# Attention products of four steps issued together instead of two, with twelve transposed-weight tiles and a smaller arena

## The chip, the cores and the metric

The kernel runs on one core of a Trainium2 chip. The metric is device time in microseconds (us) from the start to the end of one launch, taken as the median of several runs. Names of engines are those of the profile: PE is TensorE's matmul, PEld its weight loads, DVE is VectorE, ACT is ScalarE, POOL is GpSimd, SP is SyncE, whose queue issues most of the transfers.

## What is computed

Four transformer blocks follow one another on x of 8 batches x 112 tokens x 256 channels. All read the same context of 8 x 375 x 192. Cut to what matters (layer norms, biases and residual sums are in each part):

```python
def attention(x, ctx, wq, wk, wv, wo, bo):            # 16 heads
    q, k, v = heads(x @ wq), heads(ctx @ wk), heads(ctx @ wv)
    attn = softmax(einsum('bhid,bhjd->bhij', q, k) * scale)
    return merge(einsum('bhij,bhjd->bhid', attn, v)) @ wo + bo
# blocks 0 and 1: heads of 64 channels
h = h + attention(ln1(h), ln1(h), ...)                # self, 112 keys
h = h + attention(ln2(h), context, ...)               # cross, 375 keys
h = h + (lin * gelu(gate)) @ w2                       # feed-forward, 2 x 1024 wide
# block 2: cross attention alone, heads of 64 channels
# block 3: heads of 16 channels: masked self attention, masked cross attention, MLP of 1024
```

Everything is in 32-bit floats.

## The kernel before

Tokens lie as 896 rows in seven tiles of 128. Stages are numbered: 0 self, 1 cross, 2 feed-forward (block 0); 3, 4, 5 the same for block 1; 6 the cross attention of block 2; 7 self, 8 cross and 9 MLP of block 3.

Attention is cut into 176 *steps*. A self step of blocks 0 and 1 is one batch and eight heads; a cross step is one batch and four heads. Steps 0 to 15 are stage 0, 16 to 47 stage 1, 48 to 63 stage 3, 64 to 95 stage 4. From step 96 stage 6 runs with steps of stage 7 in between, from step 138 stage 8 with the rest of stage 7. Each step is made of four pieces:

- S, the scores (L948): matmuls into a PSUM tile `s` (two buffers of two banks). Behind them stand, in program order, the softmax: maxima on DVE (L910, or L896 with a mask), exponentials on ACT (L916, L904), reciprocals on DVE, and scaling of the weights `pr` on POOL, one head at a time for 375 keys (L925), one step at a time for 112 keys (L931). Heads of 16 channels are scaled after the products instead.
- T, the transposes (L975) of `pr` into a PSUM tile `mm` (four buffers), copied by ACT or DVE into a tile `wT` (L347, L355, L981, L984): three `wT` tiles for a cross step, two for a self step of eight heads.
- PV, the products with the values (L1005): 12 matmuls for a cross step of four heads. Then the result is copied into `oT`.
- E, the second half of the exponentials where heads have 16 channels.

Scores multiply pieces of 64 rows (32 in block 3), products write 64 columns (32), and the other matmuls use the whole array of 128 x 128.

PE's order is written out by the kernel's own planner (`Plan`). A loop over the steps calls S of step i + 2, then PV, then T of step i + 1, then E of step i + 2. Between these it calls `fill`, which takes *items* from a list of other work: projections to queries and keys (L665, L687), values (L712), keys of the context (L753 and L762), values of the context (L787 and L796), output projections with the residual sum and the next layer norm (L631, L635, L566 to L576), layer-norm transposes (L597), feed-forward (L1223). An item has a cost, a due step and items it must follow, with a least distance in the planner's own clock; `pace` sets how much is taken per step, and `ready` picks the item that is due first and can go. Key and value jobs of the context are opened ahead of a step's scores and closed in the next turn. Feed-forward items must follow the scores of the segment's last step by 3 us of that clock (L1238 to L1245). The loop runs in three segments, which end at the feed-forward of block 0 (step 48), of block 1 (step 96), and at the MLP; what is left of a segment's work is placed in the next.

Queries, keys and values live in one SBUF tile, `arena`, of 128 partitions x 12224 columns. The planner gives each a range of columns (values from the top, the others from the bottom: `find`, L109) and takes it back once the last reader has been issued. An item without room is not ready. Weights go through seven buffers of their own, loaded by SP in a fixed order as buffers come free.

The core of the loop, where the change is:

```python
            if lo <= i + 2 < hi:
                plan.main(("S", i + 2))

            if lo <= i < hi and (i - lo) % 2 == 1:
                plan.main(("PV", i - 1))
                plan.main(("PV", i))
            if lo <= i + 1 < hi:
                n = steps[i + 1]
                share = left / (n + 2)
                left -= plan.fill(2 * share)
                for k in range(n):
                    plan.main(("T", i + 1, k))
```

Of the kernel before, what the change touches and what calls it, by code (L numbers as in the profile page):

```python
# [299 lines left out]
def kernel(ctx: ExitStack, tc: tile.TileContext, a: dict, out: bass.AP):  # L300
    nc = tc.nc
    PSUM = bass.MemoryType.PSUM
    RINGS = {"w": 7, "row": 2, "xn": 3}
    ARENA = 12224

    const = ctx.enter_context(tc.tile_pool(name="const", bufs=1))
    wpool = ctx.enter_context(tc.tile_pool(name="wpool", bufs=RINGS["w"]))
    rpool = ctx.enter_context(tc.tile_pool(name="rpool", bufs=RINGS["row"]))
    ppool = ctx.enter_context(tc.tile_pool(name="ppool", bufs=4))
    tpool = ctx.enter_context(tc.tile_pool(name="tpool", bufs=6))  # L310
    xpool = ctx.enter_context(tc.tile_pool(name="xpool", bufs=RINGS["xn"]))
    small = ctx.enter_context(tc.tile_pool(name="small", bufs=4))
    ps_s = ctx.enter_context(tc.tile_pool(name="ps_s", bufs=2, space=PSUM))
# [5 lines left out]

    arena = const.tile([P, ARENA], F32, name="arena")  # L320
    plan = Plan(RINGS, ARENA, lambda k: 512 if k[0] == "v" else S if k[0] == "k" and k[1] in (1, 4, 6, 8) else 4 * T)

# [806 lines left out]
    def first_of(st, b):  # L1129
        return at[(st, b, 0)]  # L1130
# [263 lines left out]
    for seg in range(3):  # L1394
        lo, hi = cuts[seg], cuts[seg + 1]

        for s in (lo, lo + 1):
            for k in plan.items[("S", s)].uses + plan.items[("PV", s)].uses:
                mk = plan.maker.get(k)
                if mk is None or plan.items[mk].done:  # L1400
                    continue
                if plan.items[mk].begin is not None:
                    plan.require(mk)
                else:
                    plan.drain(mk)
        for i in range(lo - 2, hi):
            plan.step = i
            left = plan.pace(i, seg)
            plan.close_jobs()
            if lo <= i + 2 < hi:  # L1410
                plan.main(("S", i + 2))

            if lo <= i < hi and (i - lo) % 2 == 1:
                plan.main(("PV", i - 1))
                plan.main(("PV", i))
            if lo <= i + 1 < hi:
                n = steps[i + 1]
                share = left / (n + 2)
# [3 lines that stand above are left out]
                    left -= plan.fill(min(left, share))  # L1422
            if ("E", i + 2) in plan.items and lo <= i + 2 < hi:
                plan.main(("E", i + 2))
            plan.fill(left)
            plan.open_jobs(1 if i + 1 >= first_of(8, 0) else 2, i + 3.5, seg)
# [38 lines left out]
```

## Time and profile before

| what | value |
|---|---|
| time, median of 3 runs | 1659.37 us (1658.89 to 1661.41) |
| the profiled execution | 1662.19 us, its span 1660.3 us |
| PE busy | 1635.5 us, 99% of the span |
| PEld, DVE, ACT, POOL busy | 1143.1, 809.9, 782.9, 719.6 us |
| scores, transposes, products on PE (L948, L975, L1005) | 211.7, 235.4, 179.5 us |
| scaling of the weights on POOL (L925) | 384 x 1.241 us |
| mean granted PE clock | 0.997 |

The span is the time from the first to the last instruction of one profiled execution. "Busy" of PE counts overlapping matmuls once, and their ends are modelled. A row of the timeline gives the start, the length from there to the last end, the engine, the line of the code, the operation, output and inputs, and after an x the number of instructions; in square brackets stands how long the engine was idle ahead of it and what ended the idle time. A 32-bit matmul leaves two records on PE, a transpose one. A row of a table by stretch gives the stretch, its length, busy time of PE, PEld, DVE, ACT and POOL with the number of instructions, the granted PE clock (1 is full speed), the busy share of the transfer engines, and GB/s.

### The profile page before, as it was taken

How to read it: one execution, taken by the hardware profiler on the slowest of the kernel's cores; microseconds unless marked ns; L12 is line 12 of the kernel's file. 1: busy time of each engine (PE TensorE's matmuls, PEld its weight loads, DVE VectorE, ACT ScalarE, POOL GpSimd, SP SyncE). 2: the span in 40 equal slices, each digit the busy share in tenths (PEclk: the TensorE clock that was granted, in tenths of full speed). 3: DMA queues.
4: the chain of work that ended last, by engine and by line, in shares of the span. 5: the costliest groups of instructions: out<-in, count | busy, mean ns of one | idle time of the engine just before them, and what ended most of it. 6: DMA issues, size and time to landing. Idle time of an engine off the chain costs nothing.

```text
span 1660.3 us, 30115 instructions
## 1 busy us (share of the span) xinstructions
PE 1635.5 (99%) x11772; PEld 1143.1 (69%) x11772; DVE 809.9 (49%) x2163; ACT 782.9 (47%) x2450; POOL 719.6 (43%) x689
## 2 busy tenths in 40 slices
PE   8999999999999999999999999999999999999999
PEld 7877666666666878676666665666666666766667
DVE  3444445444532244544454552244455556678752
ACT  3554344444431444444444452144445555687772
POOL 1323455646631233355565580364564447422110
PEclk9999999999999999999999999999999999999999
DMA  5012020000101011000000010100000000000000
GB/s 187 5 50 57 3 87 1 1 26 1 51 30 45 1 30 52 27 1 30 1 2 26 1 46 29 33 22 2 1 2 1 16 1 27 30 2 2 2 2 23
DMA packets 26566, 39.50 MB, mean 24 GB/s; under 512 B 1544, under 2 KB 21560, under 8 KB 26424
## 3 DMA queue, kind: packets, MB, share of 16 engines
q1 hardware_dynamic: 25495, 36.74, 7.0%
q8 instruction: 93, 1.52, 0.4%
q10 hardware_dynamic: 864, 0.79, 0.2%
q14 instruction: 50, 0.40, 0.1%
q0 software_dynamic: 64, 0.05, 0.0%
HBM read 35.88 MB, written 0.92 MB: 22 GB/s over the span
## 4 chain that ended last, share of the span: by engine, by line
PE 91%; ACT 3%; DVE 3%; POOL 2%; issue 1%; DMA 0%; ACTq 0%; DVEq 0%; POOLq 0%
PE mm L631 13%; PE mm L665 11%; PE mm L1005 10%; PE s L948 10%; PE mm L975 10%; PE mm L753 8%; PE mm L787 7%; PE mm L1223 6%; PE mm L762 5%; PE mm L796 4%; PE mm L712 4%; ACT pr L904 2%; PE mm L1258 2%; POOL pr L925 1%; PE mm L597 1%
## 5 line engine op out<-in xcount | busy, mean ns | idle before, releaser
L925 POOL TENSOR_SCALAR pr<-pr,rinv 112x375 f32<-112x375 f32 x384 | 468.7, 1241 | 335.9 <-DVE rinv L922 335.7
L916 ACT ACTIVATE pr<-s,nm 112x375 f32<-112x375 f32 (+1 forms) x640 | 302.0, 489 | 168.7 <-DVE nm L910 166.5
L355 DVE COPY arena<-mm 128x375 f32<-128x375 f32 (+4 forms) x187 | 111.9, 608 | 295.4 <-PE mm L762 137.5
L975 PEld LDWEIGHTS mm<-ident,pr 112*128 112x128 f32 (+2 forms) x1920 | 209.3, 151 | 52.3 <-issue 20.9
L975 PE MATMUL mm<-ident,pr 112*128 112x112 f32 (+2 forms) x1920 | 235.4, 264 | 8.6 <-ACT pr L904 3.3
L910 DVE TENSOR_REDUCE nm<-s 112x2 f32<-112x750 f32 (+1 forms) x224 | 206.3, 957 | 70.6 <-PE s L948 67.2
L347 ACT COPY arena<-mm 128x375 f32<-128x375 f32 (+4 forms) x181 | 94.0, 519 | 298.6 <-PE mm L762 139.6
L948 PE MATMUL s<-arena 64*112 64x375 f32 (+3 forms) x1792 | 211.7, 394 | 0.1
L1005 PEld LDWEIGHTS mm<-wT,arena 128*64 128x64 f32 (+5 forms) x3840 | 159.9, 129 | 36.9 <-issue 21.2
L347 ACT COPY wT<-mm 128x448 f32<-128x448 f32 (+2 forms) x232 | 122.3, 535 | 122.6 <-PE mm L975 122.6
L1005 PE MATMUL mm<-wT,arena 128*64 128x112 f32 (+5 forms) x3840 | 179.5, 261 | 0.0
L948 PEld LDWEIGHTS s<-arena 64*112 64x112 f32 (+1 forms) x1792 | 114.0, 173 | 80.5 <-issue 31.2
L931 POOL TENSOR_TENSOR pr<-pr,rinv 112x896 f32<-112x896 f32 x32 | 53.9, 1684 | 210.5 <-DVE rinv L929 199.6
L904 ACT ACTIVATE pr<-pr,nm 112x112 f32<-112x112 f32 (+1 forms) x256 | 124.7, 490 | 33.5 <-DVE nm L896 33.5
L916 ACT ACTIVATION_READ_ACCUMULATOR pr<-s,nm 112x1 f32 x640 | 133.3, 208 | 0.0
L572 POOL TENSOR_TENSOR rs<-ve,mhalf 128x1 f32<-128x1 f32 x70 | 39.6, 567 | 193.0 <-DVE ve L570 192.8
L922 DVE RECIPROCAL rinv<-sums 112x1 f32<-112x1 f32 x384 | 62.3, 162 | 89.8 <-ACT pr L916 89.3
L787 PE MATMUL mm<-L_xattn_Wv,ctxA 128*128 128x512 f32 (+1 forms) x192 | 92.2, 600 | 2.0 <-ACT wT L347 1.3
L753 PE MATMUL mm<-ctxA,L_xattn_Wk 128*128 128x375 f32 x256 | 92.5, 485 | 0.0
L635 DVE TENSOR_TENSOR x<-mm,x 128x256 f32<-128x256 f32 x70 | 29.6, 422 | 113.7 <-PE mm L631 113.7
L665 PE MATMUL mm<-hT,L_xattn_Wq 128*128 128x224 f32 x384 | 84.1, 363 | 0.1
L355 DVE COPY wT<-mm 128x448 f32<-128x448 f32 (+2 forms) x120 | 73.6, 613 | 16.7 <-PE mm L975 16.3
(135 smaller groups left out, 2296.3 us busy)
## 6 DMA issues: line engine op xcount, KB each, us to landing
L_xattn_Wo<-in_L_xattn_Wo_dram SPq DMA_DIRECT2D x3, 1024.0 KB, 16.7
L_xattn_w_ff<-in_L_xattn_w_ff_dram SPq DMA_DIRECT2D x3, 1024.0 KB, 5.2
L_xattn_Wv<-in_L_xattn_Wv_dram SPq DMA_DIRECT2D x4, 512.0 KB, 6.0
L_xattn_Wq<-in_L_xattn_Wq_dram SPq DMA_DIRECT2D x2, 1024.0 KB, 4.7
L_xattn_Wp<-in_L_xattn_Wp_dram SPq DMA_DIRECT2D x2, 1024.0 KB, 5.7
L_xattn_wq<-in_L_xattn_wq_dram SPq DMA_DIRECT2D x2, 1024.0 KB, 4.7
L_xattn_wo<-in_L_xattn_wo_dram SPq DMA_DIRECT2D x2, 1024.0 KB, 5.5
L_xattn_mlp_w<-in_L_xattn_mlp_w_dram SPq DMA_DIRECT2D x2, 1024.0 KB, 5.2
```

Source lines behind the costliest of these rows:

```text
L347: nc.scalar.copy(dst, src)
L355: nc.vector.tensor_copy(dst, src)
L631: nc.tensor.matmul(ps[:, :D], lhsT=oT[:, c, t * P : (t + 1) * P], rhs=got[wv or w][:, c, :], start=(c == 0), stop=(c == n - 1),)
L665: nc.tensor.matmul(ps[:, i * 2 * T : (i + 1) * 2 * T], lhsT=got[w][:, k, m * P : (m + 1) * P], rhs=hT[:, k, lo:hi], start=(k == 0), stop=( ...
L753: nc.tensor.matmul(ps[:, :S], lhsT=got[wv][:, (2 * u + i) * P : (2 * u + i + 1) * P], rhs=ctxA[:, cols], start=True, stop=False,)
L787: nc.tensor.matmul(ps[: KCH[c][1], :], lhsT=lhs(ctxA, slice(0, KA), c), rhs=got[w][:, hf * 512 : (hf + 1) * 512], start=True, stop=False,)
L910: nc.vector.tensor_reduce(nm[:, :, :ns], sv, AX.X, ALU.max, negate=True)
L916: nc.scalar.activation(pr[:, bk, sl, :], sv[:, bk, sl, :], AF.Exp, bias=nm[:, bk, sl : sl + 1], accum_out=sums[:, bk, sl : sl + 1],)
L925: nc.gpsimd.tensor_scalar_mul(pr[:, bk, sl, :], pr[:, bk, sl, :], rinv[:, bk, sl : sl + 1])
L948: nc.tensor.matmul(tiles[i][:, n % 2, (n // 2) * nk : (n // 2 + 1) * nk], lhsT=qap(h), rhs=kap(h), start=True, stop=True,)
L975: nc.tensor.transpose(pt[:kl, m * T : (m + 1) * T], cell[h][:, c * P : c * P + kl], ident[:T, :T])
L1005: nc.tensor.matmul(po[p0 : p0 + dp, blk * T : (blk + 1) * T], lhsT=got[vk][:kl, hv * dp : (hv + 1) * dp], rhs=wt, start=(c == 0 and par(h) ...
```

## The change

Products of a step are no longer issued in each second turn of the loop. They are collected in a list, which is emptied when it holds four steps, at the end of a segment, and, from the first step of stage 8 on, in each second turn as before. `wT` gets twelve buffers instead of six, and the arena gets 9536 columns instead of 12224. Nothing that is computed changes.

```diff
-    ARENA = 12224
+    ARENA = 9536
...
-    tpool = ctx.enter_context(tc.tile_pool(name="tpool", bufs=6))
+    tpool = ctx.enter_context(tc.tile_pool(name="tpool", bufs=12))
...
+        waiting = []
         for i in range(lo - 2, hi):
             plan.step = i
             left = plan.pace(i, seg)
...
             if lo <= i + 2 < hi:
                 plan.main(("S", i + 2))
 
-            if lo <= i < hi and (i - lo) % 2 == 1:
-                plan.main(("PV", i - 1))
-                plan.main(("PV", i))
+
+            if lo <= i < hi:
+                waiting.append(("PV", i))
+                if len(waiting) == 4 or i + 1 == hi or (i >= first_of(8, 0) and (i - lo) % 2 == 1):
+                    while waiting:
+                        plan.main(waiting.pop(0))
             if lo <= i + 1 < hi:
                 n = steps[i + 1]
```

## The prediction

> **What bounds the kernel now.** I read the page's busy times and chain first, to see which engine sets the end.
>
> ```profile
> span 1660.3 us, 30115 instructions
> PE 1635.5 (99%) x11772; PEld 1143.1 (69%) x11772; DVE 809.9 (49%) x2163; ACT 782.9 (47%) x2450; POOL 719.6 (43%) x689
> PE 91%; ACT 3%; DVE 3%; POOL 2%; issue 1%; DMA 0%; ACTq 0%; DVEq 0%; POOLq 0%
> ```
>
> TensorE (PE) has 99% of the span and 91% of the chain. Its instructions run in the order written, so this change, which only moves work, counts in two ways: less matmul time, or more waits of PE. Next I read PE and GpSimd (POOL) in time where the first segment ends: step 47 of 176 is its last, and the feed-forward follows.
>
> ```profile
> 460.69 1.35 PE L975 MATMUL mm<-ident,pr 112*128 112x112 f32 x12
> 461.97 1.52 PE L948 MATMUL s<-arena 64*112 64x375 f32 x8
> 463.42 2.53 PE L1005 MATMUL mm<-wT,arena 128*64 128x112 f32 x48
> 465.88 0.60 PE L975 MATMUL mm<-ident,pr 112*128 112x112 f32 x4
> ...
> 474.90 1.35 PE L975 MATMUL mm<-ident,pr 112*128 112x112 f32 x12
> 476.17 2.06 PE L1005 MATMUL mm<-wT,arena 128*64 128x112 f32 x38
> ```
>
> ```profile
> 459.82 3.66 POOL L925 TENSOR_SCALAR pr<-pr,rinv 112x375 f32<-112x375 f32 x3
> 463.44 0.57 POOL L572 TENSOR_TENSOR rs<-ve,mhalf 128x1 f32<-128x1 f32 x1
> 464.13 1.23 POOL L574 TENSOR_SCALAR xn<-x,mv,rs 128x256 f32<-128x256 f32 x1
> 465.44 0.73 POOL L576 TENSOR_TENSOR x<-x,row 128x256 f32<-128x256 f32 x1
> 466.15 4.90 POOL L925 TENSOR_SCALAR pr<-pr,rinv 112x375 f32<-112x375 f32 x4
> ```
>
> Scores of step 47 (L948) end at 463.4. POOL normalizes the step before, one layer norm, then step 47's four heads, and is done at 471.05. Meanwhile PE runs the products of steps 44 and 45 (L1005), transposes of step 46 and feed-forward matmuls; step 47's transposes, at 474.90, find their input ready. Products and filler cover softmax and scaling. In all 96 cross-attention steps without mask I find the same latency: median 6.3 us from the last score to the last scaled head, 4.9 us of it four POOL scalings.
>
> Third, a step whose transposes follow its scores directly:
>
> ```profile
> 409.17 1.42 PE L948 MATMUL s<-arena 64*112 64x375 f32 x8
> 410.53 1.40 PE L975 MATMUL mm<-ident,pr 112*128 112x112 f32 x12
> 411.76 1.04 PE L787 MATMUL mm<-L_xattn_Wv,ctxA 128*128 128x512 f32 x2
> 413.04 1.13 PE L787 MATMUL mm<-L_xattn_Wv,ctxA 128*128 128x512 f32 x2 [0.24 <-DVE wT L355]
> ```
>
> Two records should take 0.86 us (429 ns each); the next starts after 1.28. It waits for a PSUM buffer, whose copy stands behind the new step's maxima and exponentials. About 0.4 us is lost here, and nothing where products or a projection stand between.
>
> Last, the granted clock around the one place where it falls after the start:
>
> ```profile
> 1374.50:1377.90 3.40, 1.89 (x14) 1.37 (x14) 2.36 (x7) 2.86 (x9) 3.40 (x4) 1.00 0.00 0
> 1377.90:1381.30 3.40, 3.40 (x10) 1.46 (x10) 0.54 (x2) 0.00 (x0) 3.40 (x3) 0.50 0.00 0
> 1381.30:1384.70 3.40, 3.40 (x52) 2.58 (x50) 2.61 (x5) 2.00 (x6) 0.66 (x2) 1.00 0.00 0
> ```
>
> After a stretch with PE busy 1.89 of 3.40 us, the clock is halved for the next 3.40. The nine matmuls there ran 1.6 us over their usual spacing.
>
> **The change part by part.** I set the matmul order of the changed program beside the old one; below, "cover" is the matmul work, at the trace's spacings, between a step's last score and its first transpose.
>
> (1) *Fewer switches of the array's tiling.* Scores, products and transposes use different tilings. Single start times show the price: last score pair to first product 405 ns against 311 inside the scores, first product pair to second 146 against 95, last product to first transpose 188 against 95, first transpose to second 152 against 96. Scores straight to transposes also pay 405 and 152, so a products group in between adds 51 + 93 = 0.145 us. The order has 495 switches before and 462 after: 33 groups fewer, **-4.8 us**.
>
> (2) *The ends of the first two segments.* Before, products of steps 44 and 45 go out after the last scores, those of 46 and 47 at the end. Now all four wait for step 47. The order there becomes: scores 46, output projection, transposes 45, scores 47, transposes 46, transposes 47, products 44 to 47, feed-forward. The planner could put no feed-forward there: its items wait for the last scores plus 3 us of its clock. Cover of step 47 falls from 11.0 us to 1.2. By the rows above: scores end at 463.4, transposes 46 (1.25 us) at 464.7. POOL's queue stands as before, the layer norm ahead of step 47, so the fourth head is ready at 471.05 and the rest of transposes 47 end at 472.0. Products take 2 x 2.47, to 477.0. The feed-forward moved behind (16 records of 0.43) and four transposes of the norm (0.44) end at 484.3; in the old trace the same work ended at 478.6. **+5.7 us**, for an idle stretch of some 6 us. Products, then norm and feed-forward are queued behind the wait, so nothing fills it. The second segment's order and POOL rows (layer norm 988.39, scaling from 991.10) are the same: another 5.7.
>
> (3) *The clock there.* 1.5 us of idle in a stretch of 3.4 halved it above, so each of these pauses must: +1.6 by that row (bounds 0.8 to 2.6, as the pause lies to the 3.4 us raster), **+3.2** for two.
>
> The Trainium skill, "TensorE: Matmul & The Clock Gate", section "Why this matters for your kernels", asks for no PE-idle gap over about 3 us, as one idle window returns the clock to half. The trace is harsher: gaps of 0.61 and 0.90 us did it. By the rule only the two segment ends are hit, by the trace also clusters of short waits in (5); the sum with the rule is the same less one 1.6.
>
> (4) *Steps with nothing between scores and transposes.* Three score steps in four now have no products. Many have a projection; but with the arena at 9536 columns the planner places keys and values later and in pairs, and in the two plain cross stages such direct steps (layer-norm transposes alone counted too) go from 4 to 12. Rows before: 0.4, 0.4, 0.7, 0.4; with a layer norm up to 1.7 (1142 to 1147 us). 8 x 0.55 = **+4.4** (bounds 2.5 to 9). One step there, number 19, has cover 5.5 for 6.3: **+0.8**.
>
> (5) *Steps 96 to 139, where two stages interleave.* By single start times the old trace loses 10 us here over its usual spacing. After, direct steps go from 6 to 13 (13 x 0.5 = 6.5). Covers under 6.3 in cross steps: 107 has 4.6, 119 6.0, 131 3.8, 135 5.3, which give 1.7 + 0.3 + 2.5 + 1.0. Step 127 (masked self attention) has 2.3 for some 4.5 (the first such step: scores end at 1256.0, the last exponential at 1260.5): 2.2. Steps 138 and 139 lose about 1.5 together, one halved clock 1.6. Sum 17.3 against 10: **+7** (bounds 0 to 16: waits in a row cover each other, or add clock windows).
>
> (6) *Costed at nothing.* From step 148 on the matmul order is the same. Twelve transposed-weight tiles hold four steps of three, so no copy waits; should one, it shows as ACT or DVE waiting for L1005. Weight loads keep their order on SP, and the seven weight buffers are untouched; a load 10 us later still meets slack. Four evacuations in a row stand behind 4.9 us of products with both copy engines free (each 0.53 or 0.61 us).
>
> Sum: -4.8 + 11.4 + 3.2 + 4.4 + 0.8 + 7 = **+22.0 us**. The profiled execution took 1662.19 with a span of 1660.3; it would become 1684.2 and 1682.3. It lay 2.8 above the median, 1659.37, from which the forecast is 1681.4; I take 1681.
>
> **Rivals.** *Only the segment ends cost.* Copies keep up in direct steps and short covers are met by waits before them: -4.8 + 14.6 = +9.8, 1669. For it: 8 of 10 direct steps before lost at most 0.7. Against: the 0.4 us came in nearly each.
>
> *The interleaved stages cascade.* POOL, with 4.9 us a step, does not catch up where scores stand 2 to 4 us apart; 16 us in (5), 9 in (4) give +35, 1695. For: that stretch already held the halved clock. Against: each wait lengthens the next cover.
>
> *Faster.* The wait of step 47 is the one thing that can carry it: were its transposes fed while products still ran, as now, (2) and (3) would be 0. With (4) and (5) hidden by other steps' longer covers (14 to 16 us in many), 4.8 remains: 1654.6. It decides once all added waits are under 4.8 us. Against: the order of transposes and products is fixed, and POOL's end at 471.05 does not move.
>
> **How the numbers follow.** Forecast 0.52 (1675 to 1688); only the ends 0.22 (1666 to 1675); cascade 0.19 (1688 to 1702); faster case 0.07 (1651 to 1665), spread over the three signs. Range 1666 to 1697: it leaves out the last and the cascade's tail. 0.2%, about 3.3 us, is what a measurement here can tell from no change: faster 0.05, same 0.03, slower 0.92.
>
> **What would show it.** Right: PE waits for POOL of some 6 us before the transposes ahead of the first two feed-forwards, each followed by a clock of 0.5; the stretch from 20 to 440 us about as long as before; the last 250 us unchanged. (1) is wrong if the first self stage, where covers stay over 9 us, is not shorter by about 0.15 us a saved group. Wrong altogether: no such pauses, or a PE wait on a weight load or on L1005.

## The result and the profile after

The changed kernel takes 1683.34 us (median of 4 runs, 1682.43 to 1685.64) against 1659.13 (1658.2 to 1661.41): ratio 1.0145, 95% interval 1.0133 to 1.0158. It is 24 us slower. The profiled execution took 1685.64 us with a span of 1683.8.

The page of the changed kernel, its span, busy times and chain:

```profile
span 1683.8 us, 29937 instructions
...
PE 1643.4 (98%) x11772; PEld 1148.9 (68%) x11772; DVE 806.7 (48%) x2166; ACT 778.6 (46%) x2447; POOL 719.4 (43%) x689
...
PE 87%; ACT 5%; DVE 4%; POOL 3%; issue 1%; DMA 0%; ACTq 0%; POOLq 0%; DVEq 0%
```

PE has the same 11772 instructions and still bounds the kernel, but its share of the chain falls from 91% to 87%. ACT, DVE and POOL have come into the chain: PE now waits for softmax.

The timeline of PE, and then of POOL, at the end of the first segment:

```profile
463.00 1.52 PE L948 MATMUL s<-arena 64*112 64x375 f32 x8
464.45 1.40 PE L975 MATMUL mm<-ident,pr 112*128 112x112 f32 x12
468.49 0.43 PE L975 MATMUL mm<-ident,pr 112*128 112x112 f32 x1 [2.64 <-POOL pr L925]
469.71 0.45 PE L975 MATMUL mm<-ident,pr 112*128 112x112 f32 x1 [0.78 <-POOL pr L925]
470.92 0.45 PE L975 MATMUL mm<-ident,pr 112*128 112x112 f32 x1 [0.76 <-POOL pr L925]
472.13 2.00 PE L975 MATMUL mm<-ident,pr 112*128 112x112 f32 x9 [0.76 <-POOL pr L925]
474.06 5.46 PE L1005 MATMUL mm<-wT,arena 128*64 128x112 f32 x96
```

```profile
464.48 0.57 POOL L572 TENSOR_TENSOR rs<-ve,mhalf 128x1 f32<-128x1 f32 x1
465.16 1.23 POOL L574 TENSOR_SCALAR xn<-x,mv,rs 128x256 f32<-128x256 f32 x1
466.48 0.73 POOL L576 TENSOR_TENSOR x<-x,row 128x256 f32<-128x256 f32 x1
467.18 4.90 POOL L925 TENSOR_SCALAR pr<-pr,rinv 112x375 f32<-112x375 f32 x4
```

The transposes of step 46 end at 465.8. Those of step 47 then come one at a time, as POOL hands over one head in 1.22 us. Before, 11 us of products, feed-forward and the transposes of step 46 stood between the scores of step 47 and its transposes; now only the transposes of step 46 are left there, and the rest is queued behind the four heads. The second segment ends in the same way, with the same four waits of PE. The granted clock in stretches behind that second end (the clock is the third value from the end of a row):

```profile
997.80:1001.20 3.40, 0.77 (x8) 0.59 (x6) 2.10 (x7) 2.64 (x9) 3.23 (x4) 0.97 0.01 2
1001.20:1004.60 3.40, 1.35 (x3) 0.55 (x3) 0.00 (x0) 0.00 (x0) 3.40 (x3) 0.50 0.00 0
1004.60:1008.00 3.40, 3.15 (x23) 2.95 (x25) 0.62 (x1) 1.06 (x2) 0.20 (x1) 0.50 0.00 0
1008.00:1011.40 3.40, 3.40 (x42) 3.40 (x41) 0.00 (x0) 0.00 (x0) 0.00 (x0) 0.52 0.02 5
1011.40:1014.80 3.40, 3.40 (x56) 3.02 (x53) 0.00 (x0) 1.47 (x3) 0.00 (x0) 1.00 0.00 0
```

The clock is halved for three stretches, 10.2 us, and only the first lies mostly over waiting; in the other two the transposes and products run, and the products take 7.00 us instead of 4.85. At the first end it was two stretches.

The trace of the kernel before holds 6.8 us of half clock near its start and 3.4 at 1378 that the traces of several experiments below lack. So stages are compared with the trace of e2, which takes the same time and lacks both.

### The profile page after: what moved, and what is told of

Its sections match the earlier page's. It is cut to its first block, busy times and chain, and to the rows that moved or that the text cites. A ratio compares the mean times of both kernels' runs of the same rounds, so it can differ in the third digit from the quotient of the medians.

```text
span 1683.8 us, 29937 instructions
## 1 busy us (share of the span) xinstructions
PE 1643.4 (98%) x11772; PEld 1148.9 (68%) x11772; DVE 806.7 (48%) x2166; ACT 778.6 (46%) x2447; POOL 719.4 (43%) x689
## 4 chain that ended last, share of the span: by engine, by line
PE 87%; ACT 5%; DVE 4%; POOL 3%; issue 1%; DMA 0%; ACTq 0%; POOLq 0%; DVEq 0%
PE mm L631 12%; PE mm L665 11%; PE mm L1005 10%; PE s L948 8%; PE mm L975 8%; PE mm L753 8%; PE mm L787 7%; PE mm L1223 6%; PE mm L762 4%; PE mm L796 4%; PE mm L712 4%; ACT pr L904 2%; POOL pr L925 2%; DVE nm L910 2%; ACT pr L916 2%; PE mm L1258 2%
## 5 line engine op out<-in xcount | busy, mean ns | idle before, releaser
L925 POOL TENSOR_SCALAR pr<-pr,rinv 112x375 f32<-112x375 f32 x384 | 468.6, 1239 | 357.9 <-DVE rinv L922 357.9
L975 PE MATMUL mm<-ident,pr 112*128 112x112 f32 (+2 forms) x1920 | 239.7, 266 | 18.7 <-POOL pr L925 13.1
L1005 PEld LDWEIGHTS mm<-wT,arena 128*64 128x64 f32 (+5 forms) x3840 | 163.2, 131 | 23.2 <-issue 11.8
L1005 PE MATMUL mm<-wT,arena 128*64 128x112 f32 (+5 forms) x3840 | 175.8, 264 | 0.0
L347 ACT COPY wT<-mm 128x448 f32<-128x448 f32 (+2 forms) x218 | 114.4, 537 | 109.8 <-PE mm L975 109.8
L931 POOL TENSOR_TENSOR pr<-pr,rinv 112x896 f32<-112x896 f32 x32 | 53.9, 1684 | 211.7 <-DVE rinv L929 205.4
L355 DVE COPY wT<-mm 128x448 f32<-128x448 f32 (+2 forms) x134 | 81.5, 610 | 54.8 <-PE mm L975 54.5
L753 PE MATMUL mm<-ctxA,L_xattn_Wk 128*128 128x375 f32 x256 | 92.2, 485 | 3.1 <-DVE wT L355 1.9
```

The lines of the kernel that those rows point to most:

```text
L347: nc.scalar.copy(dst, src)
L355: nc.vector.tensor_copy(dst, src)
L753: nc.tensor.matmul(ps[:, :S], lhsT=got[wv][:, (2 * u + i) * P : (2 * u + i + 1) * P], rhs=ctxA[:, cols], start=True, stop=False,)
L925: nc.gpsimd.tensor_scalar_mul(pr[:, bk, sl, :], pr[:, bk, sl, :], rinv[:, bk, sl : sl + 1])
L975: nc.tensor.transpose(pt[:kl, m * T : (m + 1) * T], cell[h][:, c * P : c * P + kl], ident[:T, :T])
L1005: nc.tensor.matmul(po[p0 : p0 + dp, blk * T : (blk + 1) * T], lhsT=got[vk][:kl, hv * dp : (hv + 1) * dp], rhs=wt, start=(c == 0 and par(h) ...
```

## The experiments

Each ratio is against runs of the kernel before on the same chip, whose medians lay between 1658.98 and 1659.71 us.

| run | what it is | median, us | ratio, 95% interval |
|---|---|---|---|
| e1 | fours, segment ends in pairs | 1668.10 | 1.0049, 1.0034 to 1.0064 |
| e2 | pairs, small arena | 1659.88 | 1.0001, 0.9992 to 1.0010 |
| e3 | the change, pauses filled | 1678.33 | 1.0110, 1.0093 to 1.0127 |
| e4 | the change, last step of segments scaled on DVE | 1676.92 | 1.0103, 1.0088 to 1.0118 |
| e5 | e1, groups split by a matmul | 1684.98 | 1.0150, 1.0136 to 1.0165 |
| e6 | e1, matmul behind the group | 1675.09 | 1.0094, 1.0080 to 1.0108 |
| e7 | e1, pairs where nothing else covers | 1668.87 | 1.0050, 1.0035 to 1.0064 |
| e8 | e1, pairs from step 124 | 1663.32 | 1.0021, 1.0011 to 1.0030 |
| e9 | e7, pairs from step 124 | 1661.97 | 1.0016, 1.0007 to 1.0025 |
| e10 | fours only where covered | 1660.03 | 1.0003, 0.9994 to 1.0012 |
| e11 | e4, shorter pause filled | 1672.05 | 1.0077, 1.0062 to 1.0092 |
| e12 | e7, half of the scaling on DVE | 1676.63 | 1.0105, 1.0088 to 1.0122 |

In the names, a four is the products of four steps issued together, and a pair those of two. My theory was the prediction's: two thirds of the loss at two segment ends, the rest in waits inside the stages. The main rivals were that the loss sits inside and only shows at the ends, and that the arena carries it.

**e1, the ends.**

```diff
-if len(waiting) == 4 or i + 1 == hi or (i >= first_of(8, 0) ...
+if len(waiting) == 4 or i + 1 == hi or i + 3 == hi or (i >= first_of(8, 0) ...
```

> The changed kernel, but the last four steps of a segment give out their products as two pairs, as before. My theory (the two segment ends carry two thirds of the loss, the inside of the stages the rest): by the prediction's terms (2) and (3) 14.6 us less than the changed kernel's 1683.3, so 1668.7; by the landmarks of its trace 15.6 less, 1667.7. The transposes ahead of both feed-forwards then follow products and wait for no scaling. Rival 1, the ends only show a loss that builds up in the stages, and it comes back as other waits: above 1678. Rival 2, the inside costs nothing and its delays are moved work: 1660.

Measured 1668.10, 15.2 us under the change. Both rivals fall. The timeline of PE in e1 at the same place:

```profile
462.38 1.52 PE L948 MATMUL s<-arena 64*112 64x375 f32 x8
463.83 2.53 PE L1005 MATMUL mm<-wT,arena 128*64 128x112 f32 x48
...
475.31 1.35 PE L975 MATMUL mm<-ident,pr 112*128 112x112 f32 x12
476.58 2.54 PE L1005 MATMUL mm<-wT,arena 128*64 128x112 f32 x48
```

The last transposes run in 1.35 us with no wait before them, 11.5 us behind the scores.

**e2, the arena.** The kernel before, with these two lines of the change alone:

```diff
-    ARENA = 12224
+    ARENA = 9536
-    tpool = ctx.enter_context(tc.tile_pool(name="tpool", bufs=6))
+    tpool = ctx.enter_context(tc.tile_pool(name="tpool", bufs=12))
```

> The kernel before, products in pairs, with the arena at 9536 columns and twelve wT tiles. My theory: with pairs the smaller arena moves keys and values about but leaves as many steps with nothing between scores and transposes as before (12 against 11 in stage 6 and behind, 4 in the plain cross stages as before), so 1660 (1657 to 1663): what the inside of the stages loses comes from the products that no longer stand behind scores. Rival, the late and paired placing of keys and values is what costs there, as the prediction's step (4) had it: the 6.4 to 6.8 us of the inside by the landmarks, so 1666.

Measured 1659.88. With pairs the smaller arena costs nothing that can be measured. Inside the stages it is the grouping that costs: 8.2 us between e2 and e1, which is what is left after the saved changes of tiling are taken off.

**e3, the clock.** `warm(n)` issues n matmuls of the identity matrix with itself, which nothing reads.

```diff
+                if i + 2 == hi and seg < 2:
+                    warm(24)
                 for k in range(n):
                     plan.main(("T", i + 1, k))
```

> The changed kernel with 24 identity matmuls (some 5 us of PE work that nothing reads) ahead of the last step's transposes in the first two segments, where PE waits; it adds work and computes the same. My theory: the pause stays, since scaling on POOL ends it, but the clock no longer falls: 1.6 us a segment by the prediction's step (3), 1680; by the stretches of half clock in the trace up to 3.2 for the second, 1678.5. Rival 1, the half clock in the record costs nothing by itself: 1683. Rival 2, the matmuls reach past the end of the wait: 1684 to 1688.

Measured 1678.33. The timeline of PE in e3 at the first end:

```profile
464.73 5.54 PE L376 MATMUL mm<-ident 128*128 128x128 f32 x48
470.10 0.45 PE L975 MATMUL mm<-ident,pr 112*128 112x112 f32 x3
471.18 1.12 PE L975 MATMUL mm<-ident,pr 112*128 112x112 f32 x9 [0.62 <-POOL pr L925]
472.22 4.85 PE L1005 MATMUL mm<-wT,arena 128*64 128x112 f32 x96
```

The transposes still wait for POOL, but the products take 4.85 us and the clock stays at 1.00. Matmuls that nothing reads made the kernel 5.0 us faster, so the half clock was worth that much. Of the 15.2 us of the ends 10.2 are left for the waiting itself.

**e4, POOL's queue.**

```diff
+                    eng = nc.vector if s in (47, 95) else nc.gpsimd
-                        nc.gpsimd.tensor_scalar_mul(...)
+                        eng.tensor_scalar_mul(...)
```

> The changed kernel with the scaling of steps 47 and 95 alone moved from POOL to DVE, which has little to do there. My theory: these scalings stand on POOL behind a layer norm and take 4.9 us; on DVE each follows its reciprocal, the last at 467.6 us in the trace of the changed kernel, so with a scaling of about 0.5 us (a DVE pass over 448 columns took 0.6) the weights are ready near 468.1 and not 472.1. The transposes end some 5 us sooner in each segment, 1673, and 1670 if the clock then holds. Rival, PE waits there for something else (copies, PSUM): 1682 or more.

Measured 1676.92: 6.4 us, more than the rival allows and well short of 10 to 13. PE in e4, and the clock behind the pause:

```profile
463.47 1.40 PE L976 MATMUL mm<-ident,pr 112*128 112x112 f32 x12
466.58 0.55 PE L976 MATMUL mm<-ident,pr 112*128 112x112 f32 x2 [1.71 <-DVE pr L926]
467.79 2.32 PE L976 MATMUL mm<-ident,pr 112*128 112x112 f32 x10 [0.66 <-DVE pr L926]
470.04 6.74 PE L1006 MATMUL mm<-wT,arena 128*64 128x112 f32 x96
```

```profile
464.20:467.60 3.40, 1.22 (x9) 0.77 (x7) 3.01 (x10) 2.54 (x9) 1.94 (x2) 0.94 0.00 0
467.60:471.00 3.40, 3.21 (x20) 2.87 (x22) 1.08 (x3) 1.07 (x2) 0.00 (x0) 0.50 0.00 0
471.00:474.40 3.40, 3.40 (x44) 3.40 (x42) 0.00 (x0) 0.00 (x0) 0.00 (x0) 0.56 0.00 0
```

The scores end 1.0 us earlier in this trace than in the change's, so the products start 3.0 us sooner and not 5: ahead of the scalings and between them DVE made two copies of step 46 (0.60 us each). And the clock is halved all the same, now over transposes and products: the last ten transposes take 2.32 us (1.44 in e11 below), the products 6.74 where 4.85 is usual.

**e11, the pause of e4 filled.** The edit is e3's on the kernel of e4, with warm(9).

> The kernel of e4 (steps 47 and 95 scaled on DVE) with nine identity matmuls, 2.0 us, ahead of these steps' transposes. e4 brought 6.4 us where 10 to 13 were expected; its record shows the clock at half on the products behind the pause, 6.74 and 6.07 us against 4.85. My theory, the shorter pause moved the half clock from waiting onto work: with the pause filled, 1.9 + 1.2 for products and some 1.5 for transposes come back, 1672.3. Rival, what e4 missed is something else (copies on DVE, the four products behind step 47 by themselves): 1675 or more.

Measured 1672.05; the rival falls. In e11 the products behind the shorter pause read:

```profile
463.81 2.19 PE L376 MATMUL mm<-ident 128*128 128x128 f32 x18
465.83 0.41 PE L976 MATMUL mm<-ident,pr 112*128 112x112 f32 x2
466.89 1.44 PE L976 MATMUL mm<-ident,pr 112*128 112x112 f32 x10 [0.66 <-DVE pr L926]
468.26 4.85 PE L1006 MATMUL mm<-wT,arena 128*64 128x112 f32 x96
```

So in e4 the half clock cost 4.9 us, as much as in the change, though PE was idle half as long (2.4 us against 4.9): it had moved from waiting onto work. The Trainium skill, "TensorE: Matmul & The Clock Gate", section "Why this matters for your kernels", asks for no idle gap of TensorE over about 3 us; here gaps of 1.71 and 0.66 us were enough, so the measurement is harsher than the rule.

**e5 and e6, the price of a change of tiling.**

```diff
 while waiting:
     plan.main(waiting.pop(0))
+    if four and len(waiting) == 2:      # e5
+        warm(1)
+if four:                                # e6
+    warm(1)
```

Here `four` is true for a group of four; the notes behind # are added.

> The kernel of e1 (four products together, the ends of the first two segments in pairs), with one identity matmul of the whole array, which nothing reads, in the middle of each of its 31 groups of four. It prices a change of the array's tiling: 62 more of them than in e6, which has the same matmul behind each group, between work of its own tiling. By the prediction's step (1), 0.145 us each, so 9.0 us more than e6. Rival, the spacings of single start times are taken up by the work behind them: within 2 us of e6.

> As e5, with the identity matmul behind each group of four and not in its middle. Both theories: near e1's 1668.1, with 31 matmuls of two records at some 0.11 us a record, 3 to 7 us more (1671 to 1675) or less where they fall into waits; it is there for the difference to e5.

Measured 1684.98 and 1675.09: 9.9 us for 62 changes of tiling, 0.16 us each. The rival falls, and the waits of PE behind the start of the program are the same in both traces. The traces hold 33 such matmuls, not the 31 of the expectation; the added changes are 62 all the same, since four groups change their tiling in the middle anyway (between products of 64 and of 32 columns). Over e1 the same matmul costs 0.21 us behind a group and 0.51 in its middle.

**e7, direct steps.** In a turn that has issued no products (`flushed` is set where products go out):

```diff
-                left -= plan.fill(2 * share)
+                took = plan.fill(2 * share)
+                left -= took
+                if took < 0.5 and not flushed and len(waiting) > 1:
+                    for _ in range(2):
+                        plan.main(waiting.pop(0))
```

> The kernel of e1, and where the planner has nothing (or only a layer norm's transposes) to put between a step's scores and the transposes, and two steps' products wait, they go out there. It has 485 changes of tiling (e1 464, before 495), and as few direct steps as before (2 and 2 in the first two segments where e1 has 6 and 6, 10 to 12 behind where e1 has 18 to 20). My theory, the direct steps carry the loss inside the stages: the 8.4 us of e1 go, and ten changes of tiling fewer than before are worth 1.5, so 1658.5 (1657 to 1661). Rival, it is the short covers and the late scaling of the interleaved steps, which stay as they are: 1664 or more.

Measured 1668.87. By the total my theory falls and the rival stands; the trace says more. The table gives the delay of four landmarks against e2, taken from the first exponential of a step, less the delay of step 0:

| us behind e2 | step 48 | step 96 | step 135 | end |
|---|---|---|---|---|
| e1 | 2.7 | 2.9 | 4.0 | 7.4 |
| e7 | 1.3 | 0.6 | 1.3 | 8.4 |
| e8 | 2.7 | 2.9 | 3.4 | 3.2 |
| e9 | 1.3 | 0.6 | 1.4 | 1.4 |
| e10 | 1.0 | 0.3 | 0.3 | 0.3 |

(Step 135 is the last one of stage 6. The expectations of e8 and e9 count only steps with heads of 64 channels there, which makes it "step 127". At that landmark e1 and e7 have issued 23 fewer matmul records of products than e2, one step's or some 1.2 us: so much of what follows there is work put off.)

Up to step 135, e7 gets back 2.7 of the 4.0 us. Then it loses 7.1, most of it in one place, shown here by PE and POOL in e7:

```profile
1416.75 0.26 PE L975 MATMUL mm<-ident,pr 112*128 112x112 f32 x1
1417.40 0.32 PE L975 MATMUL mm<-ident,pr 112*128 112x112 f32 x1 [0.39 <-POOL pr L925]
1418.60 0.32 PE L975 MATMUL mm<-ident,pr 112*128 112x112 f32 x1 [0.89 <-POOL pr L925]
1421.71 2.00 PE L975 MATMUL mm<-ident,pr 112*128 112x112 f32 x9 [2.79 <-POOL pr L925]
```

```profile
1414.88 3.67 POOL L925 TENSOR_SCALAR pr<-pr,rinv 112x375 f32<-112x375 f32 x3
1418.52 0.57 POOL L572 TENSOR_TENSOR rs<-ve,mhalf 128x1 f32<-128x1 f32 x1
1419.19 1.23 POOL L574 TENSOR_SCALAR xn<-x,mv,rs 128x256 f32<-128x256 f32 x1
1420.40 1.25 POOL L925 TENSOR_SCALAR pr<-pr,rinv 112x375 f32<-112x375 f32 x1
```

A layer norm has come between the third and fourth head of step 135. It is the segment end once more, on a smaller scale.

**e8 and e9, the interleaved steps.** e8 is e1 and e9 is e7 with

```diff
-(i >= first_of(8, 0) and (i - lo) % 2 == 1)
+(i >= 124 and (i - lo) % 2 == 1)
```

> The kernel of e1 with pairs again from step 124 on. Against e2's trace, e1 has lost 4.4 us by step 127 and some 3.8 in steps 128 to 139, where two stages stand side by side and transposes wait for POOL. My theory, the short covers there (3.8 us at step 131 against the 6.3 that scaling needs) make that part: 1668.1 - 3.8 = 1664.3. Rival, the loss there comes from work that fours had put off earlier, and stays: 1667 or more.

> The kernel of e7 (fours, but a pair goes out where nothing else stands between scores and transposes) with pairs alone from step 124 on. In e7's trace the first 128 steps are 1.8 us behind e2's, and then POOL makes PE wait four times, 2.8 us the longest, with the clock halved. My theory, direct steps carry the loss of the first 128 steps and short covers that of the rest: both are mended here, 1659.9 + 1.8 = 1661.7. Rival, the pause of e7 moves on to the next short cover: 1665 or more.

Measured 1663.32 and 1661.97: 4.8 and 6.9 us less than without the edit. Both forecasts come out and both rivals fall; in the table nothing is lost behind step 135 in either. e8 takes away direct steps together with short covers from step 124 on, so it doesn't tell the two apart; e9, where direct steps were mended already, speaks for the covers. Between e8 and e9 the times differ by less than their intervals separate; the landmarks say 2.0 us up to step 135, although e9 has 17 more changes of tiling, 2.7 us at 0.16.

**e10, fours where they are covered.**

```diff
-(i >= 124 and (i - lo) % 2 == 1)
+((i >= 96 or 14 <= i < 24) and (i - lo) % 2 == 1)
```

> As e9, but pairs also in steps 14 to 23 and from step 96 on: four steps' products go out together only where cover is long and something else stands between scores and transposes. 486 changes of tiling against 495 before, with no more direct steps and no shorter cover than in e2. By 0.16 us a change as e5 and e6 measured it, 1.4 us under e2 and the kernel before: 1658.3 (1657 to 1660). Rival, every four costs what it saves: 1660 to 1662.

Measured 1660.03, no difference from the kernel before. The total hardly tells the two apart (it lies 0.03 us above the one range and inside the rival's); the trace does, as it ends 0.3 us behind e2's and not ahead. The saving is there: in the second self stage e10's delay against e2 falls in equal steps from 1.02 us at step 48 to 0.56 at step 62, 0.15 for each of three groups saved. In the first it is less, 0.18 us up to step 14 and 0.33 up to step 18. But from step 18 to step 48 e10 loses 1.35. Two rows of the waits of PE in e10 that e2 doesn't have:

```profile
PE mm L975 <- ACT ctxA L347: 0.7, 1, 0.7
...
PE mm L859 <- ACT ctxA L347: 0.5, 1, 0.5
```

The context's transposes meet the copies at other moments. The timeline has these two waits at 215 and 237 us (0.47 and 0.69 us) and a third at 216 for DVE (0.19); together they come to 1.35 us, as much as was lost. That nothing else adds to it was not tested. No version here beats the kernel before.

**e12, POOL relieved.**

```diff
+                    eng = nc.vector if bk else nc.gpsimd
-                        nc.gpsimd.tensor_scalar_mul(...)
+                        eng.tensor_scalar_mul(...)
```

> The kernel of e7 (fours, pairs where nothing else stands between scores and transposes) with two of the four heads of each cross step of blocks 0 to 2 scaled on DVE (0.46 us in e4) and two on POOL, so that scaling needs some 4 us behind the scores and not 6.3. My theory, POOL's queue is what the short covers wait for: the 2 us at steps 18 to 21 and the 6 of the pause at 1417 go, 1661. Rival, 88 us more work on DVE delays maxima and copies behind them, and the steps lose as much again: 1668 or more.

Measured 1676.63, so the rival holds. The groups of the scaling in e12, on POOL and on DVE, and rows of the waits of PE that e7 lacks:

```profile
L926 POOL TENSOR_SCALAR pr<-pr,rinv 112x375 f32<-112x375 f32 x192 | 245.6, 1284 | 496.7 <-DVE rinv L922 496.5
...
L926 DVE TENSOR_SCALAR pr<-pr,rinv 112x375 f32<-112x375 f32 x192 | 86.8, 452 | 5.4
```

```profile
PE mm L787 <- DVE oT L355: 1.4, 6, 0.2
...
PE mm L753 <- DVE oT L355: 1.2, 5, 0.2
...
PE mm L631 <- DVE oT L355: 0.7, 3, 0.2
```

The pause behind step 135 went, as my theory said: between that landmark and the end e12 gains 6.1 us on e7. But steps 0 to 135 lose 14.3 on e7, and copies on DVE are late where they weren't. One place is plain: at 1149.7 us the transposes wait 1.95 us for DVE (1.33 in e7), the clock is halved for the next stretch, and eight matmuls of L753 take 4.39 us there against 2.79 in e7. The waits that the record shows do not add up to 14.3 us; what makes the rest was not settled.

## Why the prediction was right

1681 was forecast for 1683.34, and the case was the likeliest of the four.

*The ends, (2) and (3): 14.6 forecast, 15.2 measured by e1.* The order, the wait and its length came out as worked: POOL's fourth head ends 7.6 us behind the last score before and after. The split was off, and it is luck that its errors cancel. The half clock was put at 1.6 us for each pause, from one stretch of 3.4 us; it costs 5.0 for both (e3), because it lasted two and three stretches. Against e3's rows the first end loses some 1.5 us by it (products 5.46 us against 4.85, the last nine transposes 2.00 against 1.12) and the second some 3.0 (7.00 and 1.99), above the bound of 2.6. The waiting alone is 10.2, not 11.4.

That each pause "must" halve the clock was argued from a single stretch, and idle time alone doesn't settle it. The clock changes at marks that lie a whole number of 3.41 us apart within each trace. In stretches cut at these marks, without the first 12 and the last 5 us of a run, all six at full clock with PE busy for less than half (0.76 to 1.62 of 3.40 us, in the change, e4, e7 and e12) were followed by a half clock. Above that it goes both ways: after 2.22 us busy the change's own trace has it (1635.9 to 1639.3), after 1.99 e12's has not (205.4 to 208.8, with waits of 0.62 and 0.78 us in it). The two ends, at 0.76 and 0.97 us, lay far enough below.

*Fewer changes of tiling, (1): 0.145 us each forecast, 0.16 measured by e5 and e6*. The test set for it, a first self stage shorter by some 0.15 us for each saved group, is met by half: against e2 the change gains 0.19 us up to step 14, with three groups saved, and 0.33 up to step 18, with four. Steps 6 to 10 lose 0.12 there, which was not settled. In the second self stage, where nothing else moves, it is 0.15 a group: from step 50 to step 62 the delay falls from 9.78 to 9.32 us.

*Direct steps and the interleaved stages, (4) and (5), less (1): +7.4 forecast, 8.2 measured between e2 and e1.* Steps before 96 make about 3 of it and the interleaved stages 4.5 to 5, against 1.7 and 5.7 forecast (24 of the 33 saved changes lie before step 96). The waits of PE show the kind. First e2, then e1:

```profile
PE mm L753 <- DVE wT L355: 1.9, 4, 0.5
...
PE mm L975 <- POOL pr L925: 1.0, 2, 0.9
...
PE mm L787 <- ACT wT L347: 0.6, 2, 0.3
```

```profile
PE mm L975 <- POOL pr L925: 3.2, 5, 0.9
...
PE mm L753 <- DVE wT L355: 2.8, 6, 0.5
...
PE mm L787 <- ACT wT L347: 2.3, 6, 0.6
```

Waits for a copy of transposed weights ahead of key and value projections are direct steps; waits of transposes for POOL are short covers. Both grow, as forecast, by single waits of at most 0.9 us; these three rows grow by 4.8 us together.

Three things in these steps were wrong. Step (4) gave part of the cause to the arena, "the planner places keys and values later and in pairs"; e2 has that arena and loses nothing, so it takes the missing products. Whether the arena adds to it once products go out in fours is open: fours with 12224 columns were not run. Step (4) also gave step 19 and its neighbours 0.8 us; two waits there, one for POOL and one for a copy of the context's transposes, come to 2.0 by single start times, and the second kind was not thought of. And step (5) spread its 7 us over 44 steps; of the 4.5 us that e1 loses behind step 96, pairs from step 124 on (e8) take back 4.2, so nearly all of it arises there, and not over the 44 steps. In e1 the transposes of step 135 wait 0.40 and 0.89 us for POOL, whose layer norms stand ahead of its scaling.

*Costed at nothing, (6)*: PE waits ahead of no product (L1005) and for no weight load, and ACT and DVE wait for L1005 only to copy its results, never to fill `wT`. The stretch from 20 to 440 us was to be about as long as before: counted from the first exponential of step 0, that of step 46, near 455 us, comes 1.5 us later than before. The last 250 us of the profiled execution are 1.5 us longer, which was not forecast: that execution holds a half clock from 1639 to 1642 and lies 2.3 above the median.

Of the rivals, *only the segment ends* (1669) fails: the inside of the stages should then have been some 4.5 us shorter, and it is 8.2 longer. *The cascade* has its place in e7's one pause, but not in the change. *Faster* fails on the wait of step 47, and without that wait the kernel is still slower than before (e1).

## What to carry to other kernels

Work that is gathered into larger groups no longer stands where it covered something. Before gathering, find for each member what it hid, above all at the end of a stage, where everything else is queued behind the last wait: two such places cost 15 us here, while the saved changes of tiling were worth 5. Where a pause can't be avoided, it can cost more than its length, since here the clock fell and stayed low into the work behind; matmuls that nothing reads, put into the pause, won back 5 us.

## What the runs showed of the hardware

- A pause that makes the clock fall need not be long, and shortening it may win nothing at the clock: 5.0 us were lost for two pauses of some 5 us of idle time each, and 4.9 for two of 2.4. A wait of 0.62 us alone (e3) left the clock at 1.00, and so did waits of 0.62 and 0.78 us within 3.4 us (e12); 1.71 and 0.66 us halved it (e4).
- Scaling 112 x 375 values takes 452 ns on DVE and 1239 on POOL, 2.7 times as long. The Trainium skill, "GPSIMD Engine Reference", section "4.1 Engine selection", calls one-input elementwise work on GpSimd roughly line-rate; this operation (one tile, one scalar for each partition) is far from that here. With both engines at it POOL's mean rose to 1284 ns.
- A change of the array's tiling costs 0.16 us net in the middle of a stream of products, 9.9 us over 62 of them.
